# Pinning the bias matmuls, squares on GpSimd, later norms and block-wise sums in a four-layer graph network

## The chip, the cores and the metric

The kernel runs on one core of a Trainium2 chip. The metric is the device time of one execution in microseconds (us). Before the change the median of three runs is 1743.61 us (1742.4 to 1743.96). The execution that was profiled took 1743.06 us, and its span, from the first to the last instruction in the trace, is 1741.1 us.

## The reference, cut to what matters

The input is x, 8 samples of 2048 nodes with 64 features, and one 2048 x 2048 adjacency matrix A. Four layers follow one another, each as x = layernorm(x + layer(x)), all in float32:

- Layer 0: every node n has its own weights, w[n] = sum over d of embedding[n, d] * weight[d] (16 terms), for the three inputs x, A x and 2 A (A x) - x, and its own bias, embedding[n] times a 16 x 64 matrix.
- Layer 1: twice z = relu((A z) W).
- Layer 2: x W_self + (A x) W_neighbor + bias.
- Layer 3: a weighted sum of x, A x and 2 A (A x) - x (the two supports are the same matrix), and a bias.

```
out = einsum('bnki,nkio->bno', x_g, w) + b            # layer 0
x = (x - mean) / sqrt(var + eps)                      # after each layer
```

So the work is seven products of A with a 2048 x 512 matrix (8 samples of 64 features side by side), with small feature matmuls and norms between them.

## The kernel before, in words

**The first stage (lines 510 to 585)** computes A x directly. A comes in as 16 slice tiles of 1 MB, four for each of four values of `ns`, through a ring of four buffers (tag "a", line 141), loaded by the SP queue. For each `ns`, 64 matmuls of 128 x 128 by 128 x 512 (line 546, `ps_n`, two instructions each in the trace) accumulate in four PSUM banks. A warm-up of eight matmuls on an identity tile (line 516, `rise`) stands ahead of them. Beside this, `prepare` (line 452) makes sums of blocks of A on VectorE (DVE) and writes them to DRAM (`comb`) through the GpSimd (POOL) queue.

**The other six products (function `product`, line 187)** are a two-level Winograd form of the product. The outer level has seven calls of `inner`, one for each of A11, S1, A12, S2, S4, S3, A22, in this order; each `inner` has seven calls of `mul`, and each `mul` takes one 1 MB block of A (a raw block or a sum from `comb`) from the ring and issues four matmuls (eight instructions, 3.43 us). Into which PSUM bank a `mul` goes has the pattern a, b, a, b, c, b, c; there are two banks in the pool `p_mm` in layer 0, so c takes the bank that a gave up, and the next call's a and b take those of b and c. `finish(blk, ...)` adds a finished bank into a block of a C tile (tag "C", four buffers), in the order of blocks `DONE` = 0, 3, 2, 1. Sums of x quarters, T tiles (t1 to t4 at lines 292 to 309), are 2048 elements wide and take 2.28 us on DVE.

**Hand-over.** When a quarter of the result is complete, `hand_over` (line 278) queues a *feature* for each block (i, p), i the row group of four node tiles and p the pair of samples. For S3 the whole tile is summed first (`add(v, v, u)`, line 319) and the four blocks are then handed over together (line 320); the others hand over block by block from `finish`.

**The pump (class Pump, line 30).** The features are generators. After every `mul` the pump takes `rate` steps; a step resumes the first generator in the queue. `defer` keeps a generator that is to be resumed later: it counts down a gap by one per step (`tick`) and then does one piece of it; the next piece comes after the same or a second gap. `pass_mark` and `drain` empty the queue before a result is needed, and `flush` runs out what is deferred. When the queue is empty and something is deferred, a step does nothing but tick. In layer 0 the rate is 4, and a feature has eight resumptions, so a feature takes two `mul`s.

**Layer 0's feature (line 605)** forms, for four node tiles, two halves h of 12 matmul instructions (line 621, `y`, three PSUM buffers of two banks). Half 0 is evacuated by DVE with eight scalar_tensor_tensor instructions (line 629), half 1 by ScalarE (ACT) into a tile s (line 633), whose eight parts POOL then adds up (lines 638 and 640) into xy. It fetches its two inputs (tags "xT" and "tT", line 603) on the SP queue. These tags are also those of the four `eT` tiles that the bias matmuls read (line 521).

**The norm (line 331)** of two pairs is a generator of two pieces: first a square on ACT (line 352), then the chain `ss` (a reduction on DVE, line 356), lines 358 and 360, a square root on ACT (361), lines 363 to 365, and the product into xy (366). In layer 0 it is deferred with gap 4, one `mul` for each piece. `after` (line 388) defers layer 2's own terms behind layer 1's norms, with gaps of 4 and 5 and then 2, at a rate of 2.

**The order.** The kernel is written in a framework with a planner: within each engine it may place an instruction ahead of others by modelled costs and readiness, as long as dependencies hold. `tc.keep_in_program_order` takes this freedom from an instruction. The first matmul of line 546, the reduction of line 356 and, with `pin=True` (only in the product for layer 1's first half, line 688), t2 and t3 are so held. The bias matmuls (line 527, `pb`, 32 instructions; generator `biases`, queued behind the first four transposes at the start of `ns` 1) and the sum t1 (line 292) are not.

Of the kernel before, what the change touches and what calls it, by code (L numbers as in the profile page):

```python
# [10 lines left out]
AF = mybir.ActivationFunctionType  # L11
ALU = mybir.AluOpType
# [10 lines left out]
A11, A12, A22, S1, S2, S3, S4 = range(7)  # L23
# [3 lines left out]
DONE = (0, 3, 2, 1)  # L27


class Pump:  # L30
# [9 lines left out]
    def add(self, gen):  # L40
        self.jobs.append(gen)

    def defer(self, gen, gap, gap2=None, need=True):


        self.later.append([gap, gap if gap2 is None else gap2, gen, need])

    def mark(self):

# [11 lines left out]
                    pass  # L61
                self.later.remove(job)

    def tick(self):
        for job in list(self.later):
            job[0] -= 1
            if job[0] == 0:
                job[0] = job[1]
                if next(job[2], "done") == "done":
                    self.later.remove(job)  # L70

    def step(self, n=1):
        self.owed += n
        n, self.owed = int(self.owed), self.owed - int(self.owed)
        while n > 0 and (self.jobs or self.later):
            try:
                if self.jobs:
                    next(self.jobs[0])
                n -= 1
                self.tick()  # L80
            except StopIteration:
                self.jobs.pop(0)

# [7 lines left out]
def kernel(  # L91
# [18 lines left out]
    nc = tc.nc  # L110
# [6 lines left out]
    NG = N // GW  # L117
# [13 lines left out]
    pump = Pump()  # L131
# [55 lines left out]
    def product(src, feature, between=None, rate=1, own=None, pin=False):  # L187

        def quarter(h, c):

            return xy[:, h * NT // 2 : (h + 1) * NT // 2, src, c * 4 * F : (c + 1) * 4 * F]

        def add(out, a, b, op=ALU.add):
            nc.vector.tensor_tensor(out, a, b, op)  # L196
            return out

        def new_t():
            return sums.tile([P, NT // 2, 4 * F], F32, tag="T", name="T", bufs=3)  # L200

        def new_c():
            return sums.tile([P, 4, GW], F32, tag="C", name="C", bufs=4)

        def inner(q, b, finish, early=None):


            b11, b12, b21, b22 = (
                b[:, hm * TG : (hm + 1) * TG, ts(hc, 2 * F)] for hm in range(2) for hc in range(2)
            )  # L210

            def new():
                return sums.tile([P, TG, 2 * F], F32, tag="t", name="t", bufs=5)

            t1 = add(new(), b12, b11, ALU.subtract)
            t2 = add(new(), b22, t1, ALU.subtract)
            t3 = add(new(), b22, b12, ALU.subtract)
            t4 = add(new(), b21, t2, ALU.subtract)

            def mul(ps, s, xb, start, stop=True):  # L220
                a = load(q, s)
                for m in range(TG):
                    nc.tensor.matmul(  # L223
                        ps, xb[:, m, :], a[:, :, m, :], start=(start and m == 0),
                        stop=(m == TG - 1), skip_group_check=True,
                    )
                pump.step(pump.rate)

            def bank(n):
                nonlocal banks  # L230
                banks += 1
                pool = p_mm if p_mm2 is None or banks % 3 else p_mm2
                return pool.tile([P, GW], F32, tag="mm", name=f"mm{n}")

            pa, pb = bank("a"), bank("b")
            mul(pa, 0, b11, True)
            p1 = sums.tile([P, GW], F32, tag="p1", name="p1")
            nc.scalar.copy(p1, pa)  # L238
            if early is not None:
                early(2, p1)  # L240
            mul(pb, 5, t2, True)
            u2 = add(sums.tile([P, GW], F32, tag="u2", name="u2"), pb, p1)
            if early is not None:
                early(1, u2)
            mul(pa, 1, b21, False)
            finish(0, pa, None)
            mul(pb, 6, t3, False)
            u3 = add(sums.tile([P, GW], F32, tag="u3", name="u3"), pb, p1)
            if early is not None:
                early(3, u3)  # L250
            pc = bank("c")
            mul(pc, 4, t1, True)
            finish(3, pc, u3)
            mul(pb, 3, t4, False)
            finish(2, pb, p1)
            mul(pc, 7, b22, False)
            finish(1, pc, u2)

        def fresh(c):
            def finish(blk, ps, plus):  # L260
                if plus is None:
                    nc.scalar.copy(c[:, blk, :], ps)  # L262
                else:
                    add(c[:, blk, :], ps, plus)
            return finish,

        def onto(c, base, give=None):

            def early(blk, plus):
                add(c[:, blk, :], base[:, blk, :], plus)  # L270

            def finish(blk, ps, plus):
                add(c[:, blk, :], ps, (base if plus is None else c)[:, blk, :])
                if give is not None:
                    hand_over(c, *give, blk)
            return finish, early

        def hand_over(c, ih, ch, blk):
            pump.add(feature(2 * ih + blk // 2, 2 * ch + blk % 2, c[:, blk, :]))

        def prior(ih, ch):
            if own is not None:
                for blk in DONE:
                    pump.add(own(2 * ih + blk // 2, 2 * ch + blk % 2))

        b11, b12, b21, b22 = (quarter(h, c) for h in range(2) for c in range(2))


        pump.pass_mark()
        u, v = new_c(), new_c()  # L290
        inner(A11, b11, *fresh(u))
        t1 = add(new_t(), b12, b11, ALU.subtract)
        inner(S1, t1, *fresh(v))
        pump.drain()
        pump.rate = rate
        if between is not None:
            between()
        t2 = new_t()
        sub = nc.vector.tensor_tensor(t2, b22, t1, ALU.subtract)
        if pin:  # L300
            tc.keep_in_program_order(sub)
        prior(0, 0)
        c = new_c()
        inner(A12, b21, *onto(c, u, (0, 0)))
        t3 = new_t()
        sub = nc.vector.tensor_tensor(t3, b22, b12, ALU.subtract)
        if pin:
            tc.keep_in_program_order(sub)
        t4 = add(new_t(), b21, t2, ALU.subtract)
        prior(0, 1)  # L310
        prior(1, 0)
        inner(S2, t2, *onto(u, u))
        c = new_c()
        add(c, u, v)
        inner(S4, b22, *onto(c, c, (0, 1)))
        pump.mark()
        prior(1, 1)
        inner(S3, t3, *onto(u, u))
        add(v, v, u)
        for blk in DONE:  # L320
            hand_over(v, 1, 1, blk)
        inner(A22, t4, *onto(u, u, (1, 0)))

    def to_nodes(dst, pool, tiles, p, hT):
# [3 lines left out]
            nc.tensor.transpose(pt[:, k, :], hT[:, ts(k, P)], ident)  # L328
        nc.scalar.copy(xy[:, tiles, dst, ts(p, 2 * F)], pt)

    def layernorm(i, p0, n, slot, mean=False, store=False):


        cols = slice(p0 * 2 * F, (p0 + n) * 2 * F)
# [2 lines left out]
        v = xy[:, tiles, slot, cols].rearrange("p t (b f) -> p t b f", f=F)  # L337
# [10 lines left out]
        if n == 1:  # L348
            sq = sums.tile([P, TG, 2, F], F32, tag="t", name="sq1", bufs=5)
        else:  # L350
            sq = small.tile([P, TG, 4, F], F32, tag="sq", name="sq")
        nc.scalar.activation(sq, v, AF.Square)  # L352
        yield
        ss = new("ss")

# [16 lines left out]
    def then(feature, slot, single=(), gap=0, after=None, **kw):  # L372


        seen = set()

        def both(i, p, hT):
            yield from feature(i, p, hT)
            seen.add((i, p))
            if (i // 2, p // 2) in single:  # L380
                yield from layernorm(i, p, 1, slot, **kw)
            elif (i, p ^ 1) in seen:
                norm = layernorm(i, p - p % 2, 2, slot, **kw)
                if gap:
                    pump.defer(norm, gap)
                else:
                    yield from norm
                if after is not None:
                    for k in range(2):
                        pump.defer(after(i, p - p % 2 + k), 4 + k, 2, i < NG // 2)  # L390
        return both


    if True:
# [115 lines left out]
        with tc.tile_pool(name="p_n", bufs=4, space=PSUM) as p_n, tc.tile_pool(  # L510
# [13 lines left out]

            def biases():
                for t in range(NT):
                    nc.tensor.matmul(
                        pb[:, t, :], eT[t // TG][:, ts(t % TG, P)], bias0, start=True, stop=True
                    )
                    if t % TG == TG - 1:  # L530
                        yield

            for ns in range(TG):
# [6 lines left out]
                for j in range(NG):  # L540
# [17 lines left out]
                    if ns == TG - 1:  # L558
                        v = xy[:, j * TG : (j + 1) * TG, 0, :].rearrange("p t (b f) -> p t b f", f=F)
# [28 lines left out]
        if True:  # L588
# [16 lines left out]
            def feature0(g, p, hT):  # L605
# [4 lines left out]
                for k in range(TG):  # L610
# [29 lines left out]
                    nc.gpsimd.tensor_tensor(acc, acc, s[:, 0], ALU.add)  # L640
                    yield

            product(1, then(feature0, 0, gap=4), rate=4)


    late = p_z = None
# [131 lines left out]
```

## Time and profile before

| what | value |
|---|---|
| median of three runs | 1743.61 us |
| profiled execution | 1743.06 us, span 1741.1 us |
| TensorE (PE) busy | 1704.6 us, 98% of the span |
| DVE busy | 915.9 us, 53% |
| ACT busy | 279.3 us, 16% |
| POOL busy | 237.8 us, 14% |
| granted TensorE clock, mean | 0.996 |
| end of the first stage, first matmul of the Winograd products | 251.3 us |
| features of layer 0, first and last y group | 316 to 805 us |
| last PE instruction ends | 1731.2 us |

The trace gives each instruction's start and duration on its engine, and for each idle stretch the instruction of another engine, or the DMA, that ended it (the releaser). A view of waits sums these by line. The chain of work that ended last follows the releasers back from the end. A name such as `mma<-a,xy` is a matmul that writes the PSUM tile mma from tiles a and xy. "PEld" is the weight load, which overlaps with matmuls; "SPq", "ACTq" and "POOLq" are DMA issues on those queues.

### The profile page before, as it was taken

Reading aid. Unit: us, or ns where it says so; the run is one execution under the profiler, and the core shown is the slowest. Engines: PE = TensorE matmul, PEld = TensorE weight load, DVE = VectorE, ACT = ScalarE, POOL = GpSimd, SP = SyncE. Lnnn points to the kernel's source line nnn. Section 1 sums busy time; section 2 is a strip of 40 time slices with the busy share of each in tenths; the row PEclk is TensorE's granted clock in tenths of the full one; section 3 lists DMA queues with packets and bytes.
Section 4 is the critical chain, followed back from the end, with each engine's and each line's share of the span. In section 5 each row is a group of like instructions: output and inputs, shape, how many; then the busy total and the mean of one; then the engine's idle time right before and its main releaser. Section 6 shows DMA issues by size and latency. Waiting matters only on the chain.

```text
span 1741.1 us, 15541 instructions
## 1 busy us (share of the span) xinstructions
PE 1704.6 (98%) x5664; PEld 801.0 (46%) x5664; DVE 915.9 (53%) x1614; ACT 279.3 (16%) x780; POOL 237.8 (14%) x324
## 2 busy tenths in 40 slices
PE   6999999999999999999999999999999999999997
PEld 3444444444444343443445445554444455554443
DVE  4745674445545554545444255783557444453556
ACT  0000110233233223332000001121000012100001
POOL 1122100244244343442000000000000000000000
PEclk9999999999999999999999999999999999999998
DMA  9887778423422322223877777657888866678883
GB/s 321 314 326 270 253 256 292 179 85 110 168 85 100 141 97 76 88 96 152 334 279 279 286 277 259 240 209 253 292 295 291 295 227 218 233 252 310 315 309 124
DMA packets 82234, 391.18 MB, mean 225 GB/s; under 512 B 8848, under 2 KB 25232, under 8 KB 42608
## 3 DMA queue, kind: packets, MB, share of 16 engines
q1 hardware_dynamic: 70176, 346.94, 56.2%
q0 software_dynamic: 11248, 42.08, 6.6%
q10 hardware_dynamic: 736, 1.18, 0.2%
q8 instruction: 45, 0.74, 0.2%
q14 instruction: 29, 0.24, 0.0%
HBM read 339.84 MB, written 50.33 MB: 224 GB/s over the span
## 4 chain that ended last, share of the span: by engine, by line
PE 92%; DVE 4%; ACT 1%; DMA 1%; POOL 1%; issue 0%; POOLq 0%; ACTq 0%; DVEq 0%
PE mmb L223 24%; PE y L621 18%; PE mma L223 16%; PE mmc L223 15%; PE ps_n L546 13%; PE z L669 2%; PE z L699 2%; DVE ss L356 1%; PE pt L660 1%; DVE xy L629 1%; PE pt L715 1%; DVE xy L366 1%; POOL s L638 1%; ACT s L633 0%; ACT sq L352 0%; DVE C L196 0%
## 5 line engine op out<-in xcount | busy, mean ns | idle before, releaser
L223 PE MATMUL mmb<-a,t 128*128 128x512 f32 x1008 | 456.2, 595 | 0.4 <-DVE u L196 0.4
L223 PEld LDWEIGHTS mmb<-a,t 128*128 128x128 f32 x1008 | 187.4, 190 | 225.2 <-issue 222.3
L629 DVE SCALAR_TENSOR_TENSOR xy<-y,e_sb,xy 128x128 f32<-128x128 f32 x512 | 179.6, 351 | 137.3 <-PE y L621 121.3
L546 PE MATMUL ps_n<-a,xy 128*128 128x512 f32 x512 | 223.2, 594 | 0.0
L638 POOL TENSOR_TENSOR s<-s 128x512 f32<-128x512 f32 (+2 forms) x192 | 162.7, 848 | 388.8 <-ACT s L633 378.7
L633 ACT ACTIVATE s<-y,e_sb 128x128 f32<-128x128 f32 x512 | 139.0, 382 | 286.6 <-PE y L621 286.6
L223 PE MATMUL mma<-a,T 128*128 128x512 f32 x384 | 173.5, 595 | 1.7 <-DVE C L196 1.7
L196 DVE TENSOR_TENSOR u<-mmb,p 128x512 f32<-128x512 f32 x84 | 57.9, 689 | 207.8 <-PE mmb L223 207.7
L223 PE MATMUL mmc<-a,t 128*128 128x512 f32 x336 | 152.4, 596 | 2.2 <-ACT C L262 2.2
L546 PEld LDWEIGHTS ps_n<-a,xy 128*128 128x128 f32 x512 | 96.5, 191 | 115.1 <-issue 114.9
L621 PE MATMUL y<-wn,xT 64*128 64x512 f32 x512 | 136.1, 604 | 2.1 <-DVE xy L629 2.1
L621 PE MATMUL y<-wn,C 64*128 64x512 f32 x512 | 131.9, 592 | 1.5 <-DVE C L196 1.5
L223 PE MATMUL mma<-a,xy 128*128 128x512 f32 x288 | 130.8, 596 | 2.4 <-DVE C L196 1.7
L621 PE MATMUL y<-wn,tT 64*128 64x512 f32 x512 | 132.3, 593 | 0.0
L223 PEld LDWEIGHTS mma<-a,T 128*128 128x128 f32 x384 | 71.0, 190 | 87.1 <-issue 84.6
L196 DVE TENSOR_TENSOR C<-mmc,C 128x512 f32<-128x512 f32 x60 | 41.3, 688 | 105.3 <-PE mmc L223 105.3
L223 PEld LDWEIGHTS mmc<-a,t 128*128 128x128 f32 x336 | 61.8, 190 | 75.8 <-issue 71.9
L223 PE MATMUL mmc<-a,T 128*128 128x512 f32 x192 | 86.6, 594 | 0.0
L238 ACT COPY p<-mma 128x512 f32<-128x512 f32 x42 | 24.5, 584 | 386.7 <-PE mma L223 386.7
L223 PEld LDWEIGHTS mma<-a,xy 128*128 128x128 f32 x288 | 53.7, 190 | 68.6 <-issue 63.0
L621 PEld LDWEIGHTS y<-wn,xT 64*128 64x128 f32 x512 | 47.1, 187 | 72.6 <-issue 72.6
L621 PEld LDWEIGHTS y<-wn,C 64*128 64x128 f32 x512 | 50.0, 188 | 62.5 <-issue 59.9
(96 smaller groups left out, 1323.8 us busy)
## 6 DMA issues: line engine op xcount, KB each, us to landing
a<-comb SPq DMA_DIRECT2D x240, 1024.0 KB, 4.8
a<-in_blocks SPq DMA_DIRECT2D x54, 1024.0 KB, 4.8
comb<-si POOLq DMA_DIRECT2D x28, 1024.0 KB, 8.4
a<-in_slices SPq DMA_DIRECT2D x15, 1024.0 KB, 9.2
comb<-so POOLq DMA_DIRECT2D x16, 512.0 KB, 10.8
comb<-so POOLq DMA_DIRECT2D x16, 256.0 KB, 11.4
xT<-in_xT SPq DMA_DIRECT2D x16, 256.0 KB, 3.1
t1T<-hT SPq DMA_DIRECT2D x16, 256.0 KB, 2.6
```

The costliest lines, as they stand in the source:

```text
L196: nc.vector.tensor_tensor(out, a, b, op)
L223: nc.tensor.matmul(ps, xb[:, m, :], a[:, :, m, :], start=(start and m == 0), stop=(m == TG - 1), skip_group_check=True,)
L238: nc.scalar.copy(p1, pa)
L356: tc.keep_in_program_order(nc.vector.tensor_reduce(ss, sq, AX.X, ALU.add))
L366: nc.vector.tensor_tensor(v, v, rs.unsqueeze(3).to_broadcast(shape), ALU.mult)
L546: mm = nc.tensor.matmul(ps[p], xcol(0, TG * j + m, p), ch[j][:, m], start=(j == 0 and m == 0), stop=(j == NG - 1 and m == TG - 1), skip_gr ...
L621: nc.tensor.matmul(y[:, b, :], terms[n][half, ts(k, P)], wn[half, n, h * DH : (h + 1) * DH, :], start=(n == 0), stop=(n == 2),)
L629: nc.vector.scalar_tensor_tensor(acc, y[:, :, ts(d, F)], e, acc, ALU.mult, ALU.add)
L633: nc.scalar.activation(s[:, d], y[:, :, ts(d, F)], AF.Copy, scale=e)
L638: nc.gpsimd.tensor_tensor(s[:, :n], s[:, :n], s[:, n : 2 * n], ALU.add)
L669: nc.tensor.matmul(z[:, k, :], aT[:, ts(k, P)], wd[:, w, :], start=(n == 0), stop=(n == len(terms) - 1),)
L699: nc.tensor.matmul(z[n][:, k], xT[half, ts(k, P)], w[half], start=True, stop=True)
```

## The change

1. `biases`: each bias matmul is held in program order.
2. `product`: t1 (b12 - b11) is made before the call for A11 instead of after it, and where `pin` is set it is held in program order.
3. `onto` has a new hook `then(blk)`, called after a block is finished. The sum c = u + v behind S2, and v = v + u behind S3 with the hand-over of v, are made through it, block by block (512 elements each), instead of over the whole tile (2048 elements) behind the last block.
4. `layernorm` in layer 0 squares on GpSimd (a tensor_tensor product, line 352's place) instead of on ScalarE.
5. The pump: a tick in a step that found no feature in the queue counts 0.5 for the first gap of a deferred generator. With layer 0's gap of 4 and rate of 4 the first piece of a norm then comes two `mul`s behind, if the queue is empty. This holds for the deferred own terms of layer 2 as well.
6. Norms deferred in layer 0 are run out at the start of the next product only for i < 2; those with i = 2 and 3 run on by ticks, at the latest until the drain behind S1.

```diff
-    def tick(self):
+    def tick(self, idle=False):
         for job in list(self.later):
-            job[0] -= 1
-            if job[0] == 0:
-                job[0] = job[1]
+
+            job[0] -= 0.5 if idle and job[4] else 1
+            if job[0] <= 0:
+                job[0], job[4] = job[1], False
                 if next(job[2], "done") == "done":
                     self.later.remove(job)
...
-                if self.jobs:
+                idle = not self.jobs
+                if not idle:
                     next(self.jobs[0])
                 n -= 1
-                self.tick()
+                self.tick(idle)
...
                 add(c[:, blk, :], ps, (base if plus is None else c)[:, blk, :])
                 if give is not None:
                     hand_over(c, *give, blk)
+                if then is not None:
+                    then(blk)
...
         u, v = new_c(), new_c()
+        t1 = new_t()
+        sub = nc.vector.tensor_tensor(t1, b12, b11, ALU.subtract)
+        if pin:
+            tc.keep_in_program_order(sub)
         inner(A11, b11, *fresh(u))
-        t1 = add(new_t(), b12, b11, ALU.subtract)
         inner(S1, t1, *fresh(v))
...
-        inner(S2, t2, *onto(u, u))
         c = new_c()
-        add(c, u, v)
+        inner(S2, t2, *onto(u, u, then=lambda blk: add(c[:, blk], u[:, blk], v[:, blk])))
         inner(S4, b22, *onto(c, c, (0, 1)))
         pump.mark()
         prior(1, 1)
-        inner(S3, t3, *onto(u, u))
-        add(v, v, u)
-        for blk in DONE:
+
+        def last(blk):
+            add(v[:, blk], v[:, blk], u[:, blk])
             hand_over(v, 1, 1, blk)
+
+        inner(S3, t3, *onto(u, u, then=last))
         inner(A22, t4, *onto(u, u, (1, 0)))
...
-        nc.scalar.activation(sq, v, AF.Square)
+        if pool_sq:
+
+            nc.gpsimd.tensor_tensor(sq, v, v, ALU.mult)
+        else:
+            nc.scalar.activation(sq, v, AF.Square)
...
                 if gap:
-                    pump.defer(norm, gap)
+                    pump.defer(norm, gap, need=i < NG // 2)
...
                 for t in range(NT):
-                    nc.tensor.matmul(
+                    tc.keep_in_program_order(nc.tensor.matmul(
                         pb[:, t, :], eT[t // TG][:, ts(t % TG, P)], bias0, start=True, stop=True
-                    )
+                    ))
...
-            product(1, then(feature0, 0, gap=4), rate=4)
+            product(1, then(feature0, 0, gap=4, pool_sq=True), rate=4)
```

More of the change, by code (lines that the diff above doesn't have):

```diff
@@ L43, in defer @@
     def defer(self, gen, gap, gap2=None, need=True):
-        self.later.append([gap, gap if gap2 is None else gap2, gen, need])
+        self.later.append([gap, gap if gap2 is None else gap2, gen, need, True])
     def mark(self):
@@ L265, in fresh, with onto @@
             return finish,
-        def onto(c, base, give=None):
+        def onto(c, base, give=None, then=None):
             def early(blk, plus):
@@ L329, in to_nodes, with layernorm @@
         nc.scalar.copy(xy[:, tiles, dst, ts(p, 2 * F)], pt)
-    def layernorm(i, p0, n, slot, mean=False, store=False):
+    def layernorm(i, p0, n, slot, mean=False, store=False, pool_sq=False):
         cols = slice(p0 * 2 * F, (p0 + n) * 2 * F)
```

## The prediction, on record before the result

> **What bounds the kernel now.** I read the page first (busy shares), then the waits of TensorE (PE), then the timeline around each of them. PE is the bound from end to end:
>
> ```profile
> PE 1704.6 (98%) x5664; PEld 801.0 (46%) x5664; DVE 915.9 (53%) x1614; ACT 279.3 (16%) x780; POOL 237.8 (14%) x324
> ```
>
> The span is 1741.1 us, so all that an edit can win without removing matmuls lies in 36.5 us. The last PE instruction ends at 1731.2, which leaves a tail of 9.9 us (norm and stores); the rest is this list of waits, 26.7 us together:
>
> ```profile
> PE pb L527 <- DMA eT<-in_embT: 14.2, 1, 14.2
> PE mma L223 <- DVE C L196: 3.3, 2, 1.7
> PE mmc L223 <- ACT C L262: 2.2, 1, 2.2
> PE y L621 <- DVE xy L629: 2.1, 1, 2.1
> PE y L621 <- DVE C L196: 1.5, 1, 1.5
> PE pt L660 <- DVE xy L366: 1.2, 1, 1.2
> PE pt L715 <- DVE C L196: 1.0, 1, 1.0
> PE mma L223 <- ACT hT L569: 0.8, 1, 0.8
> PE mmb L223 <- DVE u L196: 0.4, 1, 0.4
> ```
>
> Over half is one wait at the start. The timeline of PE shows how it comes about:
>
> ```profile
> 14.19 3.21 PE L527 MATMUL pb<-bias,eT 16*128 16x64 f32 x14 [14.19 <-DMA eT<-in_embT]
> 17.34 3.78 PE L516 MATMUL rise<-ident 128*128 128x128 f32 x16
> 20.91 59.06 PE L546 MATMUL ps_n<-a,xy 128*128 128x512 f32 x136
> ...
> 98.82 0.43 PE L527 MATMUL pb<-bias,eT 16*128 16x64 f32 x2
> ```
>
> The planner put 14 of the 32 bias instructions ahead of everything, and their operand eT is loaded late. The warm-up, which needs only the identity tile (made by POOL at 2.4 us), and the first real matmuls stand behind them. The chain of waits in this stretch names what landed when:
>
> ```profile
> 1.18 6.44 DMA xy<-in_x
> 7.65 6.41 DMA eT<-in_embT
> ```
>
> So x's first tile was there at 7.6 us. Of the first slice of A the first part has landed by about 5.2 (SP's ninth DMA, which reuses a slot, goes out at 5.16), the last by 10.56, where DVE's first sum over it starts.
>
> The other waits lie at layer 0's boundaries. One of them on DVE, at the end of S2:
>
> ```profile
> 430.14 1.47 DVE L196 TENSOR_TENSOR t<-xy,t 128x512 f32<-128x512 f32 x1
> 434.38 1.22 DVE L356 TENSOR_REDUCE ss<-sq 128x16 f32<-128x1024 f32 x1 [2.77 <-ACT sq L352]
> ...
> 436.69 0.68 DVE L196 TENSOR_TENSOR C<-mmb,C 128x512 f32<-128x512 f32 x1
> ```
>
> The reduction ss is held in order; DVE waits 2.77 us for the square, which itself waited for POOL's last addition (433.26). Behind it the sum that frees a PSUM bank is late, and PE's next mma starts 1.66 us late at 437.42. The same happens at 573.0 (1.66). At 580.07 a feature waits 1.45 us for a C sum, behind the next product's t1, which the planner drew forward to 574.80 (2.29 us), and the 2048-wide v sum at 577.73 (2.29 us). At 673.25 the flush at the product's start has put a norm in front of 16 evacuations of y: 2.11 us, and the next 12 y instructions take 4.54 us where others take 2.6, another 1.9. At 814.25 an ACT copy stands behind a square: 2.21, and 0.38 after it.
>
> **What the Trainium skill says.** "TensorE: Matmul & The Clock Gate", Part 1, What's actually happening: the array runs at half clock until it has been busy for about 3.4 us and falls back after an idle window as long. The trace agrees on the half: 16 warm-up instructions took 3.78 us (0.236 each), 8 transposes of the same shape later 1.04 (0.13). "GPSIMD Engine Reference", section 3.1: a 2048-wide f32 tensor_tensor takes 4497 ns there, so about 2.2 us for 1024, an estimate. The trace's additions at line 638 take 1264 ns for 512 and 741 for 256, 2.04 ns per element; extended to 1024 this gives 2.31 us, which I use. Section 8: GpSimd shares SBUF interfaces with VectorE, in contention with two-input DVE instructions. The trace agrees: the sum at 430.14 took 1.47 beside a POOL addition, 0.69 alone.
>
> **The change part by part**, against the profiled execution (1743.06 us, its span and 1.96 around it).
>
> *Bias matmuls held.* They go to ns 1. Removed: the wait and the 3.21 us. The warm-up starts at about 2.5 and ends by 6.3; the first ps_n starts when x's first tile is there, 7.7 instead of 20.91: 13.2 won. Before, the first eight took 3.92 where 3.44 is normal; that 0.5 goes. New: the array idles 1.4 us after the warm-up, so its clock may fall; at worst the first 7 us run at half speed and cost 3.5, at best nothing; I take 1.5. The 14 instructions come back at full clock: eight cost 1.03 us at 107.47, so 1.7. Net **10.5** (bounds 7.5 to 13). Is it kept? The slices for j = 1, 2, 3 are there at 17.4, 22.6, 31.8 and wanted at 21.6, 35, 49 or later. The first slice of ns 1 is the tight one: its load is released by DVE (48.44), not PE, and DVE takes it at 62.88; PE would want it at about 64.3 (76.5 before). The first slice of ns 2 is released by DVE at 98.3, used at 108.3, wanted at 123. The later loads of each ns are released by PE and move with it. The later bias matmuls release eT later, whose buffers the xT loads on SP use (line 603); SP is in order, with slice loads behind, but those have 15 us in hand. Cost zero.
>
> *t1 in place.* In layer 1's first product it no longer comes at 574.80 in front of the v sum; it takes 2.29 us of DVE at A11's start, where y groups lie between the muls and DVE is free some 10 us to 5.7 needed: zero. In the other products the planner may still draw it forward. In the first, it may now stand ahead of A11's small sums, which DVE makes at 254.2 to 258.9 while PE's mmb waits for them until 258.64: 0 to 2.3, I take **1.3 lost**.
>
> *Block-wise sums.* Twelve 2048-wide sums of 2.29 (27.5 us) become 48 of 0.69 (33.1): 5.6 us more on DVE, which is at 53%. An inner then has 17 small sums, 11.7 us to PE's 24. On the path: nothing, each extra sum comes after the one that frees the bank. The v blocks become features during S3, three muls earlier: PE's y work keeps its amount and DVE's wait at 580 (1.45) goes. Their fetches on SP, and in the last product their stores, go out earlier too, ahead of loads of A; S4's blocks do so already without a PE wait, so zero (0 to 2).
>
> *Norms later, squares on POOL.* At the end of S2 the ticks are idle, so the square comes one mul later and ss too. POOL squares at 433.3 to 435.6, and ss is asked for at 435.6, with the last mul of S2. The bank needed first is then free early: 1.66 goes. The last sum of S2 stands behind ss and its 3.9 us chain, wanted at 439.0, ready at 439.0 to 440.2: **1.0 back** (0 to 2). At the end of S3 features now follow on without a pause (v's blocks), a mul takes 14 us and the square has long been done: 1.66 goes. At 673 the norms of i = 2, 3 are no longer flushed: 2.11 + 1.9 go. The last norm falls into S1's plain muls, or before; its square is off ACT, so the copy at 814 isn't behind it: 2.6 go. The eight squares occupy POOL for 18 us in a stretch where it is busy 194 of 519; two-input DVE sums beside them stretch by up to 0.8 each, 0.5 in all on the path (0 to 2). The own terms of layer 2 come up to two muls later, so the wait at 1179 (1.2) goes.
>
> Sum: 10.5 + (1.66 + 1.66 + 1.45 + 2.11 + 1.9 + 2.6 + 1.2 = 12.6) - (1.3 + 1.0 + 0.5 = 2.8) = 20.3. 1743.06 - 20.3 = 1722.8; the median stands 0.55 above the profiled execution, so **1723**.
>
> **Rivals.** (a) *The start is given back*: PE reaches ns 1 thirteen us earlier but the DMA engines are full there (share 1.00 to 1.03 in each stretch from 5 to 75 us), and a slice or an operand is late. For it: only 1.4 us in hand at 64.3. Against: 13 us in hand at the others. All lost gives 1722.8 + 10.5 + 0.55 = 1734. (b) *The norms' waits change place*: ss still stands in front of bank-freeing sums, now behind a 2.3 us square instead of 1.06. Losing the 9.8 gives 1733. (c) *Slower*: idle ticks count half and the flush no longer takes i = 2, 3, so the last norms and own terms remain until the drain behind S1, and run there in one piece, with PE waiting: in layer 0 two squares and chains (2 x 6.2) and t2 with two small sums (3.7), 16 us; in layer 2's product four own terms at some 2 us of exposed latency and 3.7 of sums, 12 us. 1723.3 + 28 = 1751. It decides from the point where the last feature ends after S1's second mul; by my count it ends in A11's sixth, with eight muls in hand. (d) *It doesn't do it*: the planner fills the gaps with other waits of the same sum, 1743.
>
> **How the numbers follow.** The forecast 0.62 (1717 to 1729 from the bounds above), (a) 0.17, (b) 0.13, (c) 0.04, (d) 0.04. Less than 1716 isn't possible: all waits but the tail gone and the start at 7.7. The range 1716 to 1735 takes in (a) and (b). A difference of 0.2%, 3.5 us, is about what a measurement of this kernel can tell from none: faster 0.92, same 0.04, slower 0.04.
>
> **What would show it.** Right: rise at about 2.5 and ps_n before 9 us, no wait at pb; all 32 pb instructions between 80 and 97; no PE wait above 1.5 us from 430 to 820; squares on POOL of about 2.3 us; t1 of layer 1's product at its start. Wrong: a wait of ps_n for slices near 64; long DVE idle before ss; a cluster of PE waits at the end of S1.

## The result and the profile after

The changed kernel takes 1724.72 us (median of five runs, 1723.09 to 1725.91), the kernel before 1743.21 us (five runs, 1742.39 to 1743.96). The ratio is 0.9893, with a 95% interval of 0.9879 to 0.9908: 18.5 us less, against 20.3 us forecast. The profiled execution has a span of 1722.9 us.

The busy line of the profile: PE does the same work, and its share has risen.

```profile
PE 1704.1 (99%) x5664; PEld 798.5 (46%) x5664; DVE 921.2 (53%) x1650; ACT 271.4 (16%) x772; POOL 258.5 (15%) x332
```

The waits of PE after the change:

```profile
PE rise L528 <- POOL ident masks.py:199: 2.5, 1, 2.5
PE ps_n L558 <- ACT hT L581: 2.1, 1, 2.1
PE mma L225 <- ACT p L240: 1.7, 1, 1.7
PE pt L672 <- DVE xy L378: 1.1, 2, 0.7
PE pt L727 <- DVE C L198: 1.1, 1, 1.1
PE mma L225 <- ACT hT L581: 0.8, 1, 0.8
```

They sum to 9.3 us where they were 26.7. The long wait at `pb` is gone, and so are those of `mma` and `y` for a C sum and of `y` for an evacuation. Three are new in the list: that of the warm-up for the identity tile, a time that before lay inside the wait for eT; that of ps_n for hT; and that of an mma for ACT's copy p.

The timeline of PE shows the new start:

```profile
2.48 3.79 PE L528 MATMUL rise<-ident 128*128 128x128 f32 x16 [2.48 <-POOL ident masks.py:199]
6.05 59.33 PE L558 MATMUL ps_n<-a,xy 128*128 128x512 f32 x136
...
71.79 5.40 PE L558 MATMUL ps_n<-a,xy 128*128 128x512 f32 x8 [2.09 <-ACT hT L581]
...
84.86 1.10 PE L539 MATMUL pb<-bias,eT 16*128 16x64 f32 x8
```

The warm-up now runs while x loads, and ps_n starts at 6.05 instead of 20.91. At 71.79 PE has waited 2.09 us, and the eight instructions behind the wait take 5.40 us where eight take 3.60 elsewhere in the stage. The windows of PE (busy us, then granted clock, DMA share, GB/s) say why:

```profile
70.00:71.80 1.80, 0.01 (x1) 1.00 1.03 406
71.80:73.60 1.80, 1.80 (x3) 0.70 1.05 369
73.60:75.40 1.80, 1.80 (x3) 0.50 1.02 323
75.40:80.00 4.60, 4.60 (x14) 0.94 0.60 206
```

After 2.1 us without work the clock fell to half for about 3.4 us: these stretches miss 1.8 x 0.30 + 1.8 x 0.50 + 4.6 x 0.06 = 1.7 us of full clock.

To see where the time went I cut each trace at three instructions: the first mma (end of the first stage), the mma at which A12 of layer 1's first product begins (end of the layer-0 stretch), and the end of the last PE instruction. This is better than the waits alone, since it also counts slow instructions and changes between kinds of matmul. The medians come from four sets of runs, in which the kernel before took 1742.3 to 1743.2 us.

| kernel | first stage | layer-0 stretch | from there to the last PE instruction | median, us |
|---|---|---|---|---|
| before | 251.26 | 574.05 | 905.9 | 1743.21 |
| changed | 242.63 | 563.46 | 907.2 | 1724.72 |
| bias matmuls held only | 242.28 | 575.04 | 905.9 | 1733.14 |
| norms only | 249.73 | 564.18 | 907.1 | 1734.37 |
| block-wise sums only | 249.90 | 564.39 | 904.8 | 1731.07 |
| t1 only | 249.60 | 576.81 | 905.9 | 1746.37 |
| changed, squares on ACT | 242.39 | 562.89 | 907.1 | 1723.53 |
| changed, norms early | 243.91 | 565.88 | 904.8 | 1726.03 |
| changed, hT in more buffers | 237.71 | 564.41 | 907.2 | 1720.69 |
| changed, no warm-up | 241.44 | 563.45 | 907.2 | 1723.28 |
| held and sums, nothing else | 242.23 | 564.40 | 904.8 | 1722.85 |
| hT, half ticks for norms only | 236.61 | 564.41 | 904.8 | 1718.29 |
| the same, squares on ACT | 237.68 | 563.86 | 904.8 | 1716.42 |
| the same, t1 behind A11 | 237.22 | 562.42 | 904.8 | 1715.42 |

The change won 8.6 us in the first stage and 10.6 in layer 0, and lost 1.3 behind it. The first column varies by itself: the wait for eT at the start was 14.2 us in the profile of the kernel before and 13.1 to 13.2 in three others that start alike, and their first stages end at 249.6 to 249.9 instead of 251.3. Against those three, the first stage won 7.0 to 7.3 us. A wait is named below by the time at which it ended in the kernel before (437, 573, 580, 673, 814 and 1179 us), whatever its time in the kernel at hand.

### The profile page after: what moved, and what is told of

The parts are those of the page before. It is cut to its first block, busy times and chain, and to the rows that moved or that the text cites. A ratio compares the mean times of both kernels' runs of the same rounds, so it can differ in the third digit from the quotient of the medians.

```text
span 1722.9 us, 15569 instructions
## 1 busy us (share of the span) xinstructions
PE 1704.1 (99%) x5664; PEld 798.5 (46%) x5664; DVE 921.2 (53%) x1650; ACT 271.4 (16%) x772; POOL 258.5 (15%) x332
## 4 chain that ended last, share of the span: by engine, by line
PE 95%; DVE 3%; DMA 1%; ACT 0%; POOL 0%; issue 0%; POOLq 0%; ACTq 0%
PE mmb L225 25%; PE y L633 19%; PE mmc L225 16%; PE mma L225 16%; PE ps_n L558 12%; PE z L681 2%; PE z L711 2%; DMA t1T<-hT 1%; PE pt L672 1%; PE pt L727 1%; DVE ss L368 0%; PE pt_n L336 0%; DVE sm L352 0%; DVE xy L353 0%; DVE xy L378 0%; PE pb L539 0%
## 5 line engine op out<-in xcount | busy, mean ns | idle before, releaser
L650 POOL TENSOR_TENSOR s<-s 128x512 f32<-128x512 f32 (+2 forms) x192 | 167.0, 870 | 349.9 <-ACT s L645 339.9
L633 PEld LDWEIGHTS y<-wn,tT 64*128 64x128 f32 x512 | 49.9, 187 | 60.3 <-issue 60.3
## 6 DMA issues: line engine op xcount, KB each, us to landing
comb<-so POOLq DMA_DIRECT2D x16, 512.0 KB, 11.4
```

Of the source, the lines that this page charges most:

```text
L633: nc.tensor.matmul(y[:, b, :], terms[n][half, ts(k, P)], wn[half, n, h * DH : (h + 1) * DH, :], start=(n == 0), stop=(n == 2),)
L650: nc.gpsimd.tensor_tensor(s[:, :n], s[:, :n], s[:, n : 2 * n], ALU.add)
```

## The experiments

The first four each make one part of the change in the kernel before. In all four the kernel before took 1742.47 us (17 runs).

**Bias matmuls held, alone.**

```diff
-                    nc.tensor.matmul(
+                    tc.keep_in_program_order(nc.tensor.matmul(
                         pb[:, t, :], eT[t // TG][:, ts(t % TG, P)], bias0, start=True, stop=True
-                    )
+                    ))
```

> The kernel before with the bias matmuls held, and nothing else. Theory (the gain has two independent parts, 8.6 us in the first stage and 10.6 us in layer 0): the first stage ends at about 242.6 instead of 251.3 and the time is 1734.6 us. Rival (PE's lead is taken back later, as layer 0's waits don't shrink with it): first stage shorter, but the time stays above 1738 us.

Measured: 1733.14 us, ratio 0.9947 (0.9934 to 0.9959). The first stage ends at 242.28, and layer 0's waits are those of before, but for the last one of 0.4. The layer-0 stretch is 1.0 us longer, since this time the clock fell to half (0.50 from 805.3 to 808.6) at the wait of 814, which it had not done in the kernel before. The start's gain is kept to the end and needs nothing of the rest.

**Norms alone** (half ticks, narrower flush, squares on GpSimd).

```diff
+            job[0] -= 0.5 if idle and job[4] else 1
...
+                    pump.defer(norm, gap, need=i < NG // 2)
...
+            nc.gpsimd.tensor_tensor(sq, v, v, ALU.mult)
```

> The kernel before with the squares on GpSimd, the half ticks and the narrower flush; sums, t1 and bias matmuls as before. Theory (the norms' chain on DVE made the waits): the waits at 437, 673 and 814 go (1.66 + 4.0 + 2.6), the one at 573 too (1.66), one of up to 1.7 comes back, so 9 us less: 1734 us. Rival (it is the early hand-over of v that removes the waits at 573 and 673): only 437 and 814 go, 4.3 us less, 1739 us.

Measured: 1734.37 us, ratio 0.9952 (0.994 to 0.9965). The layer-0 stretch falls by 9.9 us: the waits at 437, 573, 673 and 814 are gone without any earlier hand-over, a wait of 1.2 for a C sum stays, and one of 1.1 us for a block from `comb` comes. The theory held, and the rival (only two of the waits go) didn't. The half ticks and the narrower flush were not taken apart. Behind layer 0 this kernel loses 1.2 us (907.1 for 905.9), as the whole change does.

**Block-wise sums alone.**

```diff
-        inner(S2, t2, *onto(u, u))
         c = new_c()
-        add(c, u, v)
+        inner(S2, t2, *onto(u, u, then=lambda blk: add(c[:, blk], u[:, blk], v[:, blk])))
...
-        inner(S3, t3, *onto(u, u))
-        add(v, v, u)
-        for blk in DONE:
+        def last(blk):
+            add(v[:, blk], v[:, blk], u[:, blk])
             hand_over(v, 1, 1, blk)
+        inner(S3, t3, *onto(u, u, then=last))
```

> The kernel before with the block-wise sums alone. Theory: only the wait of 1.45 us at 580 and perhaps that of 1.66 at 573 go, 1740.5 to 1742 us. Rival (the early hand-over makes layer 0's gain): the waits at 573 and 673 go as well, 6 to 7 us less, 1736.5 us.

Measured: 1731.07 us, ratio 0.9932 (0.9919 to 0.9944), 11.4 us less. Here my theory failed and the rival was right. The waits of PE in this kernel:

```profile
PE pb L530 <- DMA eT<-in_embT: 13.2, 1, 13.2
PE mma L223 <- DVE C L196: 1.3, 1, 1.3
PE pt L718 <- DVE C L196: 1.1, 1, 1.1
PE mma L223 <- ACT p L238: 0.8, 1, 0.8
PE mma L223 <- ACT hT L572: 0.8, 1, 0.8
```

The norms are as early as before and on ACT, yet the waits at 573 and 673 are gone. With v's blocks handed over during S3, features follow without a pause from S4 to the next product's A11. A norm then has 14 us beside it (a `mul` and the y matmuls that follow it). At the start of the next product the norm's reduction, at 701.04, comes behind the evacuations of y, in front of which it had stood, and the last feature ends 535.5 us after the first mma instead of 553.7. Only at the end of S2, where no feature is handed over earlier, does a wait of 1.3 us remain. The wait of 1179 in layer 2's part is gone as well, which is the 1.1 us of the third column.

**t1 ahead of A11, alone.**

```diff
+        t1 = new_t()
+        sub = nc.vector.tensor_tensor(t1, b12, b11, ALU.subtract)
+        if pin:
+            tc.keep_in_program_order(sub)
         inner(A11, b11, *fresh(u))
-        t1 = add(new_t(), b12, b11, ALU.subtract)
```

> The kernel before with t1 ahead of A11, pinned in layer 1's first product, and nothing else. Theory: the wait at 580 goes or halves, nothing else moves, 1742 to 1743.5 us. Rival (t1 ahead of A11's small sums makes PE wait at the products' starts): 1745 us and a new wait at 255 or 680.

Measured: 1746.37 us, ratio 1.002 (1.0012 to 1.0028), slower by 3.9 us. The wait at 580 went, as I expected, and that of 673 grew, about where the rival had put a new one (680). DVE in this kernel, at the start of layer 1's first product:

```profile
663.11 1.22 DVE L359 TENSOR_REDUCE ss<-sq 128x16 f32<-128x1024 f32 x1 [2.28 <-ACT sq L355]
...
666.95 2.29 DVE L292 TENSOR_TENSOR T<-xy 128x2048 f32<-128x2048 f32 x1
669.15 0.34 DVE L632 SCALAR_TENSOR_TENSOR xy<-y,e_sb,xy 128x128 f32<-128x128 f32 x1
669.41 1.49 DVE L196 TENSOR_TENSOR t<-T 128x512 f32<-128x512 f32 x1
670.83 5.62 DVE L632 SCALAR_TENSOR_TENSOR xy<-y,e_sb,xy 128x128 f32<-128x128 f32 x15
```

The held t1 stands behind the flushed norm and in front of the evacuations of y. PE waits 5.6 us for these, where it waited 2.1. The table shows 2.8 us of the 3.9, in the layer-0 stretch; the profiled execution is the fastest of 13.

The next four undo or add one thing in the changed kernel (the kernel before took 1742.74 us beside them, seven runs).

**Squares back on ACT.**

```diff
-            product(1, then(feature0, 0, gap=4, pool_sq=True), rate=4)
+            product(1, then(feature0, 0, gap=4), rate=4)
```

> The changed kernel with the squares of layer 0 back on ScalarE, still two muls behind. Theory (lateness does it, the engine doesn't): within 1 us of the changed kernel, 1724 us; the ACT copy of p at 788 may come later by the square's 1.06. Rival (ScalarE was the obstacle): the copy behind a square costs 2 us or more again, 1727 us or above.

Measured: 1723.53 us, ratio 0.989 (0.9873 to 0.9906). The layer-0 stretch is 0.6 us shorter, and the wait of mma for p falls from 1.7 to 0.8. So it is not the move to GpSimd that helped.

**Norms one mul behind again** (full ticks, flush for all).

```diff
-            job[0] -= 0.5 if idle and job[4] else 1
+            job[0] -= 1
...
-                    pump.defer(norm, gap, need=i < NG // 2)
+                    pump.defer(norm, gap, need=True)
```

> The changed kernel with full ticks and the flush for all norms, so that the norms come one mul behind; squares still on GpSimd. Theory: the wait at the end of S2 comes back, larger since the square takes 1.9 us on GpSimd (about 2.5), and one of that kind behind the last feature; nothing at S3's end or at the start of A11, where v's early blocks keep the features running: 1727 to 1730 us. Rival (the lateness matters at each boundary): 1734 us.

Measured: 1726.03 us, ratio 0.9905 (0.989 to 0.992). The wait at the end of S2 is back with 2.2 us, none at S3's end or at the start of A11: as the theory had it. The time is below the 1727 to 1730 us expected, for the last stretch is 2.3 us shorter (904.8), which I had not foreseen.

**hT of pairs 2 and 3 in tag t.**

```diff
-                    hT = sums.tile([P, GW], F32, tag=f"u{2 + p % 2}", name="hT")
+                    hT = sums.tile([P, GW], F32, tag=f"u{2 + p % 2}" if p < 2 else "t", name="hT", bufs=1 if p < 2 else 5)
```

> The changed kernel with the first stage's hT of pairs 2 and 3 in the five buffers of tag t, so that they don't wait for the write of pairs 0 and 1 to DRAM. Theory (the 2.09 us wait at 71.8 and the slow 8 instructions behind it, 1.8 us, come from that buffer): the first stage ends near 238.7 and the time is 1721 us. Rival (the DMA engines are full there and PE waits for the next slice instead): 1724.7 us with a wait for in_slices.

Measured: 1720.69 us, ratio 0.9874 (0.986 to 0.9889). Both waits for hT are gone, no wait for slices came in their place, and A12 of layer 1 starts at 802.12 instead of 806.09: 4.0 us, the 2.09 of the wait and the 1.8 of slow clock. The reader should look at ACT in the changed kernel, where the copy of pair 2 stands behind the write of pair 0 to DRAM, which uses the same buffer:

```profile
71.15 0.59 ACT L581 COPY hT<-ps_n 128x512 f32<-128x512 f32 x1 [15.44 <-DMA t1T<-hT]
```

The two writes issued from 52.3 on took 19.0 us (median) to land; in the kernel before two such writes in that place took 8.8. The DMA engines were full in both (a share of 1.01 to 1.05 from 52 to 72 us here, 1.01 from 67 to 72 there), so that alone doesn't make the difference. Here three loads of slices had been issued just ahead of the writes, from 47.96 to 51.45; that these held them up is likely, but not shown.

**No warm-up.**

```diff
-            for k in range(8):
+            for k in range(0):
```

> The changed kernel without the eight warm-up matmuls. Theory (they warm the clock while x loads): the first ps_n still start near 6 but run at half clock for 3.4 to 7 us, 1.7 to 3.5 us lost, 1727 us. Rival (the clock follows the first ps_n anyway, or the start isn't held by x): no difference, 1724.7 us, or ps_n start earlier.

Measured: 1723.28 us, ratio 0.989 (0.9875 to 0.9905): no difference, though the theory was right about the start. The first line of PE here:

```profile
5.28 25.22 PE L558 MATMUL ps_n<-a,xy 128*128 128x512 f32 x51 [5.28 <-DMA xy<-in_x]
```

51 instructions at 0.43 us are 21.9, so 3.3 us are lost: until 11.4 us the weight loads come 0.85 us apart, then 0.43, as if the clock were at half (the clock record of this trace shows 1.00 there). The first transposes come at 66.81 instead of 65.22. But then the wait for hT is 1.0 us and the clock doesn't fall behind it, and at 76.27 this kernel starts the products that the changed one starts at 77.46. What the warm-up wins at the start is given back at hT; whether it would be kept in the kernel without that wait was not run.

The last four (kernel before 1742.32 us, nine runs) test what this left open.

**Bias matmuls held and block-wise sums, nothing else** (the first and third diff above).

> The kernel before with the bias matmuls held and the block-wise sums; norms, ticks, flush, squares and t1 as before. Theory (these two parts bring all of the gain, since early features leave the norms' waits behind, and the later own terms of layer 2 cost 2.3 us): 8.6 + 9.7 + 1.1 us less than before, about 1723 us, no slower than the changed kernel. Rival (the norms' lateness is needed beside the sums): 1727 us or above, with waits of 1.5 us or more at S2's end and in S1.

Measured: 1722.85 us, ratio 0.9888 (0.9874 to 0.9901): 19.5 us less than the kernel before beside it, where the whole change had 18.5. Two of its parts bring all of its gain.

**Half ticks for layer 0's norms alone**, with hT in more buffers.

```diff
-                    pump.defer(norm, gap, need=i < NG // 2)
+                    pump.defer(norm, gap, need=i < NG // 2, slow=True)
...
-        self.later.append([gap, gap if gap2 is None else gap2, gen, need, True])
+        self.later.append([gap, gap if gap2 is None else gap2, gen, need, slow])
```

> The kernel with hT in five buffers, and the half ticks only for layer 0's norms, so that layer 2's own terms come as early as before. Theory (those terms, later by up to two muls, cost the stretch behind layer 0 2.3 us, in two waits and in more changes between kinds of matmul): 1718.4 us, no wait at the transposes of line 672. Rival (the 2.3 us come from the way the sums shift work between the stretches): 1720.7 us.

Measured: 1718.29 us, ratio 0.9859 (0.9846 to 0.9873). The last stretch falls from 907.2 to 904.8 us and the wait of the transposes is gone, so the half ticks of layer 2's own terms cost 2.3 us. One group of the own terms' matmuls shows in its busy time that it stands in smaller pieces between the products: first the changed kernel, then the one with early norms, whose line this kernel has too.

```profile
L711 PE MATMUL z<-w2o,xT 64*128 64x128 f32 x256 | 18.1, 283 | 0.0
```

```profile
L711 PE MATMUL z<-w2o,xT 64*128 64x128 f32 x256 | 17.5, 281 | 0.0
```

Counted over the whole last stretch, from each PE instruction's start to the next one's and without the waits, the changed kernel takes 905.0 us in 253 pieces of one kind (products, transposes, or the matmuls of one weight), this kernel 903.8 us in 245. The waits there are 2.2 and 1.1 us. Together that is the 2.3 us.

**Also squares on ACT** (the diff above).

> The same as the half ticks for norms only, with the squares of layer 0 on ScalarE. Theory (the square is 1.06 us there and 1.9 on GpSimd, and DVE's chain behind the last feature starts that much sooner): 0.6 to 0.9 us less, 1717.6 us. Rival (no difference): 1718.4 us.

Measured: 1716.42 us, ratio 0.985 (0.9837 to 0.9864); the layer-0 stretch 0.55 us shorter, as before. The medians differ by 1.9 us; the two profiled executions do not show the rest.

**Also t1 behind A11 and free.**

```diff
-        t1 = new_t()
-        sub = nc.vector.tensor_tensor(t1, b12, b11, ALU.subtract)
-        if pin:
-            tc.keep_in_program_order(sub)
         inner(A11, b11, *fresh(u))
+        t1 = add(new_t(), b12, b11, ALU.subtract)
```

> The last kernel with t1 behind A11 and free again, as in the kernel before. Theory (t1's place costs 3 us only where the flush puts a norm in front of it; with early features it does neither good nor harm): within 1 us of the last kernel, 1717 to 1718.5 us. Rival (t1 in place is needed against the wait at 580): 1.5 us more and a wait of a y matmul for a C sum. Third case (t1's place costs here as well): 2 us or more less, 1715.5 us.

Measured: 1715.42 us, ratio 0.9844 (0.9831 to 0.9857), the fastest kernel of all, some 9 us below the changed one. The layer-0 stretch is 1.4 us shorter. Its waits of PE:

```profile
PE rise L525 <- POOL ident masks.py:199: 2.5, 1, 2.5
PE pt L724 <- DVE C L198: 1.1, 1, 1.1
PE mma L225 <- ACT p L240: 0.8, 1, 0.8
```

The C sum at 580 isn't waited for, though t1 is as free as it was. The runs of the two kernels don't overlap (1716.31 to 1717.55, 1715.06 to 1716.08). The medians differ by 1.0 us, at the edge of what the theory allowed and half of the third case. No wait of PE differs by as much between them; the order of the matmuls does. With t1 ahead of A11, three pairs of y matmuls stand alone among the first products:

```profile
242.15 1.12 PE L633 MATMUL y<-wn,xT 64*128 64x512 f32 x2
...
246.84 1.12 PE L633 MATMUL y<-wn,xT 64*128 64x512 f32 x2
...
258.38 1.12 PE L633 MATMUL y<-wn,tT 64*128 64x512 f32 x2
```

With t1 behind A11 only one does, at 241.69. Such a pair takes 1.05 us to the start of the next product, where two y matmuls within a feature take 0.44, and the eight product instructions behind it take 3.63 us instead of 3.43. Two pairs fewer are worth 1.6 us by this count, which covers the 1.4. So it is the order chosen by the planner that costs here; the changed kernel, with t1 in place too, has one lone pair.

## Why the prediction was right, and where it was not

The forecast was 1723, and 1724.72 was measured. The frame held: PE is the bound, the gain is the sum of its waits, and the start and layer 0 count separately. Four terms of the sum were off, and partly cancelled: the start brought 1.9 us less than forecast, layer 0 2.0 more, and the stretch behind it lost 1.3 where 1.2 were to be won. That the sum came within 2 us is in part luck. Two of the signs named for a right forecast did not come: one PE wait between 430 and 820 us is above 1.5 (1.68, at 788.82), and the last bias matmuls end at 99.9 instead of by 97. And the lower bound of 1716 was no bound: it took ps_n's start for fixed at 7.7, and the last kernel above, with further edits, takes 1715.42.

**The start (10.5 forecast; 8.6 measured, 7.0 to 7.3 against the three profiles with the shorter wait for eT).** The mechanism was right. ps_n starts at 6.05, not 7.7: I took the landing of 7.6 in the chain for that of x's first tile, but without the warm-up the first ps_n goes at 5.28 and is named as waiting for x. The slow clock that I feared behind the warm-up cost little, as ps_n follows the warm-up without idle time: the 136 instructions take 0.3 us more than before, where I had taken 1.5 less 0.5. The bias matmuls came back for 1.03 us a group of eight, as priced. What failed is the sentence that the gain is kept with zero cost. I compared slices with their use and found one with 1.4 us in hand; that one was in time. I left out the writes of hT to DRAM, whose two buffers PE needs back when it reaches ns 1 earlier: 2.09 us, and 1.8 of slow clock. (14.9 won at the first ps_n, less 0.3, less 1.8 for 14 bias matmuls, less 3.9 at hT, is 8.9.) Rival (a) had the place and the full DMA engines, with the wrong transfer.

**Layer 0 (12.6 less the wait of 1.2, less 2.8 in new costs: 8.6 forecast, 10.6 measured).** The waits of 437, 573, 580 and 673 are gone, and that of 814 shrank. The last sum of S2, for which I took 1.0 back, cost nothing: there the chain of the norm is split by the planner. DVE and POOL in the changed kernel:

```profile
425.30 2.22 POOL L362 TENSOR_TENSOR sq<-xy 128x1024 f32<-128x1024 f32 x1
...
425.69 2.37 DVE L198 TENSOR_TENSOR C<-C 128x512 f32<-128x512 f32 x1
...
427.99 1.21 DVE L368 TENSOR_REDUCE ss<-sq 128x16 f32<-128x1024 f32 x1
...
429.61 0.63 DVE L198 TENSOR_TENSOR C<-mmc,C 128x512 f32<-128x512 f32 x1
```

The bank-freeing sum at 429.61 is put inside the chain, ahead of the norm's last four DVE instructions, and ends at 430.24; PE wants the bank at 430.65. The 1.3 I took for A11's small sums was not lost either: mmb starts at 253.73, 11.1 us after the first mma instead of 7.4, but y matmuls fill the gap and PE doesn't wait. What remains of the 2.6 us of 814 is 1.68 where mma waits for ACT's p at 788.82. I had reasoned that with its square off ACT the norm could no longer hold up a copy there. But its square root is still on ACT, and the copy stands behind it:

```profile
788.08 0.21 ACT L373 ACTIVATE rs<-rs 128x16 f32<-128x16 f32 x1 [6.97 <-DVE rs L372]
788.20 0.57 ACT L240 COPY p<-mma 128x512 f32<-128x512 f32 x1
```

The root waits for DVE's chain, and that for the GpSimd square (784.40 to 786.29). The waits and the slow clock of layer 0 were 11.4 us by my sum, so 9.7 of the 10.6 are explained; the other 0.9 lies between the starts of matmuls that wait for nothing, and was not traced.

**Who did it.** I gave the norms' lateness most of layer 0's gain and the block-wise sums 1.45 with a share in 573. Alone, either gives nearly all (9.9 and 9.7 us), together 10.6 with t1's cost in it. So the step "at 673 the norms of i = 2, 3 are no longer flushed" was true but not needed. Rival (b) is out: in layer 0 of the changed kernel no PE wait is for a sum.

**Layer 2's own terms (1.2 gain forecast, 1.3 loss measured).** The sums alone take the wait at 1179 away (904.8 us behind layer 0, for 905.9). With the half ticks it became two of 0.4 and 0.7, and the matmuls stand in smaller pieces (907.2), so that the half ticks cost 2.3. This step had the wrong sign. Rival (c), a cluster at the drain, didn't come: no PE wait ends there in S1 but the 1.68.

**t1 (1.3 lost in the first product, zero elsewhere).** Made alone, it costs 3.9 us, since I had costed its place with y's slack but not with the flushed norm ahead of it. In the whole change that norm no longer stands there, and what t1's place costs in it was not measured by itself; in the last kernels it is 1.0 us by the medians and 1.4 in the layer-0 stretch, by the order of the matmuls and not by the sum.

**The square on GpSimd** takes 1.895 us (median of eight, 2.22 at most), not 2.31; the page of the Trainium skill, "GPSIMD Engine Reference", section 3.1, led to 2.2. I took 0.5 us for its contention with DVE sums. The squares on GpSimd do cost 0.6 us (the run with squares on ACT), but the trace shows another reason: the wait for p is 1.68 with them and 0.79 without. The agreement is luck.

## What to carry to other kernels

Where one engine is busy all the time, list its waits and price each; but when two edits can each remove the same wait, only runs of one part alone tell which is needed, and the one left over may cost. When an engine gets ahead in a stage in which the DMA engines are full, look at the buffers that writes hold, not only at the loads it will want. A deferral made for one consumer should not be given to all: the half tick meant for the norms scattered another layer's matmuls.

## What the runs showed of the hardware

- A DVE sum with two SBUF inputs, 0.69 us alone, took 2.37 at 425.69, beside a GpSimd square that ran from 425.30 to 427.52: it ended 0.5 us after the square. The Trainium skill, "GPSIMD Engine Reference", section 8, names the contention; here the sum was held for most of the GpSimd instruction.
- Short idle times of PE can halve its clock. In the 14 traces, the clock record behind the start shows half clock for 3.41 us, or twice that, at five of five waits of 2.50 to 5.61 us and at four of seven of 2.09 to 2.22 us (at 71.8 in the changed kernel and at 673 in the one before, where 2.30 us at 0.65 and 2.30 at 0.60 follow; not at 814 there). No wait of 1.68 us or less shows it. The Trainium skill, "TensorE: Matmul & The Clock Gate", gives an idle window of about 3.4 us; here less was enough, sometimes.
- Two y matmuls (64 rows of weights) alone between products (128 rows) took 1.05 us to the next product's start, and 0.44 within a feature.
- A write of 256 KB to DRAM took 8.8 us to land in one kernel and 19.0 in another (medians of two), with the DMA engines full in both. What made the difference is not shown.
